# A two-layer MetaFormer kernel: three of layer 0's 56 expert tiles stand in a branch

## Chip, cores and metric

The kernel runs on one core of a Trainium2 chip. The metric is the device time of one execution in microseconds (us), as a median of several runs. Engines are named as in the profile: PE (TensorE matmul), PEld (its weight load), DVE (VectorE), ACT (ScalarE), POOL (GpSimd), SP (SyncE, which here issues nearly all plain DMAs). A q behind a name (POOLq) is that engine's sequencer.

## What is computed

The reference is a network of two layers on an input x of shape 2 x 256 x 56 x 56. Each layer adds a token mixer and then a mixture of experts. Layer 0's mixer is a windowed attention, layer 1's a pair of ternary 3x3 convolutions with batch norm. The change touches only layer 0's mixture of experts, in which every one of the 6272 tokens goes to two of eight experts:

```python
logits = tokens @ router_w.T
probs = softmax(logits)
rw, re = top_k(probs, 2)             # two experts per token
rw = rw / max(rw.sum(-1), 1e-12)
combine = zeros(N, 8).at[n, re].set(rw)
out = tokens
for e in range(8):
    h = gelu(tokens @ w1[e] + b1[e])  # 256 -> 256
    y = h @ w2[e] + b2[e]             # 256 -> 256
    out = out + combine[:, e:e+1] * y
```

All inputs come from a fixed seed, so the number of tokens that each expert gets is fixed too.

## The kernel before

**The tiles.** The router writes each token's row (and its number) twice to a DRAM tensor `xs`, into the region of its expert, by an indirect DMA. The experts then work on tiles of G = 256 rows of one expert. How many tiles an expert needs is known only from the counts, so the program has a fixed number of tile bodies, NTILE = (2·6272 + 8·255) // 256 = 56, which is enough for any counts. Which expert and which rows a body works on is read at run time from a table `where`. The table is made in two parts: part 0 (27 tiles, `EARLY[0]`) from the counts of the first strips, part 1 (29 tiles) when all counts are known. `planning` makes part 1 on DVE; in it, `end` holds the running sum of tiles over the experts, so that its last entry is the number of tiles that part 1 needs. Bodies beyond the last needed tile are executed all the same: their mask `held` is zero everywhere, the target row of every row becomes `FAR`, and the scatter with its bounds check writes nothing.

**One tile** is five steps in `experts_in_order`. `fetch_rows(j)`: SP reads a register from `where` and loads 256 rows (`xg`). `fetch_weights(j)`: SP reads a register and loads the expert's two weight matrices and biases (`w`, 641 KB; four buffers). `turn(j)`: PE transposes the rows into `pt`, ACT copies them to `ut`; DVE makes the target rows `dest` and `to`. `first(j)`: PE multiplies into `ph` (L1187), ACT applies the GELU to get `h` (L1194). `second(j)`: PE multiplies into `py` (L1206), DVE adds the bias to get `y` (L1216), and POOL scatters two blocks of 128 rows into `ys` by indirect DMA (L1218).

**The order.** The loop over tiles is software-pipelined by hand: rows are fetched four tiles ahead, weights three, `turn` two and `first` one. The order written in the source is the order on SP, PE, DVE and ACT (`manual_schedule` over these four engines); POOL's instructions are placed by the framework's scheduler, in their data order. After each tile the loop calls `beside(j)`, which advances other work that is hidden beside the experts: the ternary quantization of layer 1's convolution weights (`ternary`, DVE and ACT, L1402 to L1413), and, at j = NTILE - 2, three loads of `x_mid` (L1829) for the next stage.

**Behind the tiles** comes the start of layer 1. `combine(i)` gathers for strip i the two expert outputs of each token from `ys` (`got`, L1254), adds them up with the gates (L1270 on DVE; L1263 and L1266 on ACT and POOL for one strip), normalizes and transposes, and the first convolution (L1928) starts. The gathers read all of `ys`, so the first of them waits for the last scatter.

At its very end the kernel has one branch already: `either` reads a flag on every engine (L2401) and jumps over a general fallback program (L2402) if the flag is 0, which it is here.

## Time and profile before

| | |
|---|---|
| median of 3 runs | 1740.41 us (1736.08 to 1745.44) |
| the profiled execution | 1737.13 us, of which the span from first to last instruction is 1735.3 us |
| granted TensorE clock, mean | 0.899 |
| PE busy | 1507.6 us (87% of the span) |
| DVE / ACT / POOL busy | 957.5 / 692.9 / 636.8 us |
| experts of layer 0, first to last `py` | 505.4 us to 789.6 us |
| first `got` of layer 1's start | issued at 794.97 us |

The profile gives for each engine a list of instructions with start and duration, and for each idle stretch what ended it. The stage table gives, for chosen stretches of time, each engine's busy time, the granted clock and what the DMA engines moved. A busy engine is not by itself a bound: what a change in one stage is worth is read from the chain of waits there.

### The profile page before, as it was taken

What the parts mean: (1) busy time and instruction counts of PE and PEld (TensorE: products, weight loads), DVE (VectorE), ACT (ScalarE), POOL (GpSimd) and SP (SyncE); (2) the same over time, 40 slices, a digit from 0 to 9 for tenths busy, and PEclk for the clock granted to TensorE, in tenths of its full rate; (3) what the DMA queues carried; (4) which work ended last, traced back from release to release, by engine and by line L of the source; (5) the groups of instructions that cost most, each with busy time, mean ns of one, the idle gap of its engine ahead of it and who ended that gap; (6) DMA issues with size and microseconds to landing.
All of it is one profiled execution on the core that took longest, in us unless ns stands there. A gap on an engine that the chain in (4) does not pass through costs nothing. (4 is left out here: it accounts for less than half of the span.)

```text
span 1735.3 us, 25573 instructions
## 1 busy us (share of the span) xinstructions
PE 1507.6 (87%) x8445; PEld 1176.0 (68%) x8445; DVE 957.5 (55%) x2620; ACT 692.9 (40%) x1419; POOL 636.8 (37%) x728
## 2 busy tenths in 40 slices
PE   5999998999878788894989879957769999999964
PEld 3555565556557667783768768746658888888852
DVE  3456667466635335885999888777622212111136
ACT  2544443444323324544444263235423334343323
POOL 2111436235333653552333323427715542222210
PEclk9999999999879999996999989955579999999975
DMA  7112334112257769794441000024357777888858
GB/s 241 42 64 90 111 102 145 60 62 80 80 181 248 249 203 322 258 331 176 170 170 70 1 1 0 10 65 141 126 198 274 271 258 262 282 288 288 293 198 317
DMA packets 94157, 291.78 MB, mean 168 GB/s; under 512 B 20151, under 2 KB 35611, under 8 KB 84928
## 3 DMA queue, kind: packets, MB, share of 16 engines
q1 hardware_dynamic: 70384, 231.82, 40.3%
q0 software_dynamic: 19824, 51.82, 7.9%
q10 hardware_dynamic: 3808, 6.42, 1.0%
q8 instruction: 69, 1.13, 0.3%
q14 instruction: 72, 0.59, 0.1%
HBM read 218.55 MB, written 74.20 MB: 169 GB/s over the span
## 5 line engine op out<-in xcount | busy, mean ns | idle before, releaser
L1187 PE MATMUL ph<-ut,w 128*128 128x256 f32 (+1 forms) x1472 | 311.8, 363 | 18.5 <-DMA w<-in_L_experts 10.0
L1216 DVE TENSOR_TENSOR y<-py,w 128x512 f32<-128x512 f32 (+1 forms) x120 | 76.8, 640 | 412.5 <-PE py L1206 341.4
L1206 PE MATMUL py<-w,h 128*128 128x256 f32 x1288 | 300.5, 381 | 3.4 <-DVE y L1216 2.5
L1187 PEld LDWEIGHTS ph<-ut,w 128*128 128x128 f32 x1472 | 251.4, 195 | 49.6 <-DMA w<-in_L_experts 10.3
L1206 PEld LDWEIGHTS py<-w,h 128*128 128x128 f32 x1288 | 244.5, 192 | 37.1 <-DVE y L1216 2.9
L934 POOL DMA_INDIRECT xs<-u,pos x196 | 194.0, 990 | 127.9 <-issue 43.1
L1218 POOL DMA_INDIRECT ys<-y,dest x136 | 137.0, 1008 | 233.0 <-DVE dest L1162 100.4
L1194 ACT ACTIVATE h<-ph,w 128x256 f32<-128x256 f32 (+1 forms) x368 | 162.6, 448 | 119.0 <-PE ph L1187 91.5
L1597 ACT ACTIVATE ex<-sc 112x476 f32<-112x476 f32 (+3 forms) x224 | 116.9, 573 | 177.6 <-PE sc L1587 169.8
L1159 ACT COPY ut<-pt 128x512 f32<-128x512 f32 (+1 forms) x120 | 65.1, 543 | 293.1 <-PE pt L1155 258.2
L1928 PE MATMUL pc<-lo,wq 128*128 128x448 f32 x336 | 131.8, 394 | 5.7 <-DVE lo L1903 5.4
L1617 DVE TENSOR_TENSOR acc<-av,acc 128x238 f32<-128x238 f32 (+3 forms) x224 | 88.1, 408 | 82.9 <-PE av L1607 74.7
L1928 PE MATMUL pc<-hi,wq 128*128 128x448 f32 x336 | 131.0, 392 | 2.5 <-DVE x L1950 1.9
L1607 PE MATMUL av<-ex,vals 112*64 112x238 f32 (+3 forms) x896 | 126.9, 407 | 4.0 <-DVE acc L1617 4.0
L1218 POOL DMA_INDIRECT ys<-y,to x81 | 81.7, 1009 | 121.9 <-DVE dest L1162 63.4
L2071 PE MATMUL pc<-hi,wq 128*128 128x448 f32 (+1 forms) x288 | 102.5, 366 | 18.1 <-ACT hi L2038 9.4
L1578 PE MATMUL sc<-q_im,keys 32*112 32x238 f32 (+3 forms) x896 | 99.2, 423 | 7.9 <-ACT ex L1597 7.8
L2071 PE MATMUL pc<-lo,wq 128*128 128x448 f32 (+1 forms) x288 | 101.8, 363 | 0.2 <-DVE lo L2039 0.2
L1155 PE MATMUL pt<-ident,xg 128*128 128x128 f32 x434 | 71.2, 285 | 33.6 <-DMA xg<-xs 25.5
L1901 POOL TENSOR_TENSOR v<-pad 128x928 f32<-128x928 f32 (+1 forms) x28 | 56.7, 2035 | 103.5 <-ACT pad L1884 59.5
L1607 PEld LDWEIGHTS av<-ex,vals 112*64 112x64 f32 x896 | 57.3, 143 | 53.5 <-issue 30.0
L1155 PEld LDWEIGHTS pt<-ident,xg 128*128 128x128 f32 x434 | 56.5, 148 | 48.8 <-DMA xg<-xs 22.5
(278 smaller groups left out, 2474.5 us busy)
## 6 DMA issues: line engine op xcount, KB each, us to landing
w<-in_L_experts SPq DMA_DIRECT2D x64, 1154.0 KB
w<-in_L_experts SPq DMA_DIRECT2D x56, 641.0 KB
xg<-xs SPq DMA_DIRECT2D x97, 260.0 KB
acc<-in_fresh SPq DMA_DIRECT2D x14, 896.0 KB
got<-ys SPq DMA_DIRECT2D x21, 512.0 KB
got<-ys SPq DMA_DIRECT2D x7, 1024.0 KB
xt<-in_x_tok SPq DMA_DIRECT2D x14, 448.0 KB
rec<-shares SPq DMA_DIRECT2D x28, 224.0 KB
```

The source lines that it names most:

```text
L934: w = nc.gpsimd.indirect_dma_start(xs[:, :], bass.IndirectOffsetOnAxis(ap=pos[:, j, t0 + t : t0 + t + 1], axis=0), at_of[t][0][:, at_of[t] ...
L1155: nc.tensor.transpose(pt[:, k, i * P : (i + 1) * P], d["xg"][:, i, k * P : (k + 1) * P], ident)
L1187: nc.tensor.matmul(ph[:, :g], w1[:, k, f * P : (f + 1) * P], d["ut"][:, k, :g], start=k == 0, stop=k == KC - 1,)
L1194: nc.scalar.activation(d["h"][:, f, :g], ph[:, :g], AF.Gelu, bias=b1[:, f : f + 1])
L1206: nc.tensor.matmul(py[:, i, :], d["h"][:, f, i * P : (i + 1) * P], w2[:, f, :], start=f == 0, stop=f == NF - 1,)
L1218: o = nc.gpsimd.indirect_dma_start(ys[:, :], bass.IndirectOffsetOnAxis(ap=d["to"][:, i : i + 1], axis=0), y[:, i, :], None, bounds_check=T ...
L1578: nc.tensor.matmul(sc[h // 2][:, h % 2, :nq], keys[g][p, c, tx * TT : (tx + 1) * TT], q_im[p, c, r0:r1, c0:c1], start=True, stop=False,)
L1597: nc.scalar.activation(e[:, :, :nq], sc[j][:, :, :nq], AF.Exp, scale=HD**-0.5)
L1607: nc.tensor.matmul(av[VW * i : VW * (i + 1), :nq], vals[g % 3][:, tx, 2 * c + j, 2 * i : 2 * i + 2, :].rearrange("p a d -> p (a d)"), ex[j ...
L1617: added = nc.vector.tensor_tensor(d, av[:, :nq].rearrange("p (h w) -> p h w", w=c1 - c0), d, ALU.add)
L1928: nc.tensor.matmul(pc[:, :NT], wq[:, k, c, dx * C + o * P : dx * C + (o + 1) * P], part[:, :, k, dx : dx + W], start=m == 0, stop=m == 2 * ...
L2071: nc.tensor.matmul(pc[:, : 2 * ns * W], wq[:, k, c, dx * C + o * P : dx * C + (o + 1) * P], part[:, : 2 * ns, k, dx : dx + W], start=m == ...
```

## The change

The loop over layer 0's tiles stops after 53 of the 56 bodies. The last three stand in a branch behind it, written without the software pipeline. A new one-element tile `spare` is computed in `planning`: it is 1 if part 1 needs more than 29 - 3 = 26 tiles, that is, if the counts reach the 54th tile. Every engine reads `spare` into a register and branches on it. If the branch isn't taken, each engine runs a short block of semaphore operations in its place (each engine waits that its own earlier work is done and then adds to its semaphores what the three tiles would have added), so that later waits see the same counts either way. The three loads of `x_mid` move from j = 54 to j = 51.

```diff
+SPARE = 3
@@ in planning
             end = table("end", E)
             nc.vector.tensor_reduce(end, ends, AX.X, ALU.add)
+            if part == 1 and not halves:
+                spare = rt.tile([1, 1], I32, tag="spare", name="spare", bufs=1)
+                nc.vector.tensor_scalar(
+                    spare, end[0:1, E - 1 : E], float(n - SPARE), None, ALU.is_gt
+                )
+                spares.append(spare)
             yield
@@ in experts
             steps = experts_in_order(layer, FF, plans, ys, wp, at_tile)
             next(steps)
             steps.send((tp, ps))
+        more = nc.values_load_multi_w_load_instructions(spares[0], min_val=0, max_val=1)[1][0]
+        with tc.If(more > 0):
+            finish(steps)
@@ in experts_in_order
-        for j in range(len(tiles)):
-            if j + ROWS_AHEAD < len(tiles):
+        n = len(tiles) if layer else NTILE - SPARE
+        for j in range(n):
+            if j + ROWS_AHEAD < n:
                 fetch_rows(j + ROWS_AHEAD)
-            if j + AHEAD < len(tiles):
+            if j + AHEAD < n:
                 fetch_weights(j + AHEAD)
-            if j + 2 < len(tiles):
+            if j + 2 < n:
                 turn(j + 2)
-            if j + 1 < len(tiles):
+            if j + 1 < n:
                 first(j + 1)
             second(j)
             if at_tile is not None:
                 at_tile(*((j, 3) if layer else (j,)))
         yield
+        for j in range(n, len(tiles)):
+            fetch_rows(j)
+            fetch_weights(j)
+            turn(j)
+            first(j)
+            second(j)
@@ in beside
-            if j == NTILE - 2:
+            if j == NTILE - SPARE - 2:
                 for i in range(X_FIRST):
                     nc.sync.dma_start(XT[STRIPS[i]], by_token(x_mid, i))
```

On the engines the built program differs only around this place. SP reads `spare` right behind the planning, ahead of its first read of part 1's `where`, and branches when it has issued the `x_mid` loads. PE, DVE and ACT read `spare` and branch when their part of tile 52, the 53rd, is issued. POOL reads it and branches between the scatters of tile 51 and those of tile 52: tile 52's two scatters stand behind the branch. ACT's two copies of the ternary weights (L1413), which stood before `ut` of tile 55, stand behind the branch. The skipped block is short: 16 instructions on POOL, 14 on ACT, 19 on DVE, 45 on PE, 37 on SP. The block that the kernel's old last branch skips has 208 on POOL, 2453 on ACT, 3579 on DVE and 8261 on PE.

More of the change, by code (lines that the diff above doesn't have):

```diff
@@ L773, in scaled @@
             )
-    pace, spread = [], []
+    pace, spread, spares = [], [], []
     def routing(layer, wp, tp, ps):
```

## Prediction

> **What bounds the kernel at this place.** I read the stage table first, around the end of layer 0's tiles:

> ```profile
> core 0: us, PE busy (x) PEld busy (x) DVE busy (x) ACT busy (x) POOL busy (x), PEclk, DMA share, GB/s
> ...
> 745.00:784.00 39.00, 37.30 (x192) 32.50 (x190) 32.70 (x86) 19.73 (x36) 20.80 (x22) 1.00 0.92 315
> ...
> 784.90:794.90 10.00, 4.71 (x22) 3.80 (x20) 1.38 (x2) 0.95 (x2) 4.56 (x5) 0.95 0.02 0
> ...
> 797.00:820.00 23.00, 7.87 (x25) 4.56 (x26) 16.73 (x48) 14.32 (x32) 3.71 (x2) 0.50 0.66 260
> ```

> Up to 784 PE is the bound (37.3 of 39.0 us, clock 1.00), with the DMA engines close behind. In the ten us before 794.9 nothing is moved at all (0 GB/s), though four scatters are issued in them: the last tiles write no rows. Then comes a thin stage in which PE hardly works: DVE and ACT prepare the first strips of layer 1.

> Next the timeline of those us, engine by engine:

> ```profile
> 776.51 1.89 PE L1206 MATMUL py<-w,h 128*128 128x256 f32 x8
> ...
> 780.41 1.89 PE L1206 MATMUL py<-w,h 128*128 128x256 f32 x8
> ...
> 785.99 3.62 PE L1206 MATMUL py<-w,h 128*128 128x256 f32 x16
> ...
> 808.62 1.68 PE L1283 MATMUL pu<-ident,xn 128*128 128x128 f32 x6 [19.01 <-ACT xn L767]
> ...
> 779.50 4.12 ACT L1413 CAST sums<-x 128x2304 bf16<-128x2304 f32 x2 [2.31 <-DVE x L1410]
> ...
> 778.44 0.69 DVE L1216 TENSOR_TENSOR y<-py,w 128x512 f32<-128x512 f32 x1 [0.18 <-PE py L1206]
> ...
> 799.36 2.07 DVE L1270 SCALAR_TENSOR_TENSOR x<-got,wgt,x 128x256 f32<-128x256 f32 x5 [9.02 <-DMA got<-ys]
> ...
> 776.99 0.98 POOL L1218 DMA_INDIRECT ys<-y,to  x1 [0.30 <-issue]
> ...
> 779.41 0.97 POOL L1218 DMA_INDIRECT ys<-y,to  x1 [1.44 <-DVE y L1216]
> ...
> 780.69 0.98 POOL L1218 DMA_INDIRECT ys<-y,to  x1 [0.30 <-issue]
> ...
> 792.73 0.98 POOL L1218 DMA_INDIRECT ys<-y,to  x1 [0.30 <-issue]
> ...
> 794.97 1.29 SPq L1254 DMA_DIRECT2D got<-ys  x3
> ```

> Counting back from the end, the `py` at 785.99 is tiles 54 and 55, 780.41 is 53 and 776.51 is tile 52. The chain runs: last `y`, last scatter (ends 793.71), 1.26 us until SP may issue the gather (794.97), gather lands, DVE starts (799.36), and PE, idle for 19.01 us, starts at 808.62. So whatever moves the last scatter moves everything behind it.

> **Is the branch taken?** The counts follow from the reference's fixed inputs: the eight experts get 1527, 1691, 1588, 1573, 1468, 1602, 1515 and 1580 rows, hence 6+7+7+7+6+7+6+7 = 53 tiles. Part 1 needs 53 - 27 = 26, and 26 > 26 is false: not taken. The nearest a count comes to a step is 9 rows (1527 of 1536), far more than rounding moves. The 0 GB/s row says the same. Tile 52 holds only the last 1580 - 6·256 = 44 rows.

> **What is removed.** Three bodies, tiles 53 to 55. A body costs PE 3.9 us (776.51 to 780.41), so 11.7 us of PE; and ACT's 4.12 us `sums` copies, which delayed `ut` of tile 55, no longer stand in front of a tile. I don't add these up but take the chain: tile 52's scatters end at 780.69 + 0.98 = 781.67 in the old trace and nothing ahead of them changes. The old last one ended at 793.71. That is 12.04 us.

> **The landing.** The old last scatter was empty and took 1.26 us from its end to the gather's issue. Tile 52's carries 44 rows. Lower bound 1.26 us; upper bound 3.2 us, since all traffic had ceased by 784.9 although 1.3 MB of `x_mid` loads were in the queues with it. Those loads now come some 11 us earlier, so I take 1.5, near the lower. Gather at 783.2 in place of 794.97: 11.8 us gained.

> **The branch on each engine.** The old trace has no such short jump, but it has the kernel's last branch:

> ```profile
> L2401 POOLq TENSOR_LOAD <-flag x1: 492/492/492, 1671.7 to 1671.7; - x1
> ...
> L2402 POOLq COMPARE_BRANCH  x1: 57/57/57, 1672.3 to 1672.3; - x1
> ...
> L2402 POOLq EVENT_SEMAPHORE  x1: 17/17/17, 1672.8 to 1672.8; - x1
> ...
> L2402 DVEq COMPARE_BRANCH  x1: 72/72/72, 1727.5 to 1727.5; - x1
> ...
> L2402 DVEq EVENT_SEMAPHORE  x1: 21/21/21, 1731.1 to 1731.1; - x1
> ...
> L2402 PEldq COMPARE_BRANCH  x1: 3710/3710/3710, 1728.8 to 1728.8; - x1
> ```

> POOL, jumping over 208 instructions, has its next instruction 0.5 us after the branch; DVE over 3579 needs 3.6 us, PE over 8261 3.7 us, and ACT over 2453, in rows of the same view, 3.1 us. [...]

> - POOL is the only engine on the path: its branch stands ahead of tile 52's scatters. Its sequencer runs ahead of the engine (its last `ys` scatter in the trace starts at 1672.7, behind the branch at 1672.3). It is free at the latest when tile 51's second scatter ends, 777.97, and probably some 2 us earlier. Load 0.49, compare 0.06, jump 0.5, some four waits 0.3 and a second jump out of that block 0.1 to 0.5: 1.5 to 1.9 us, so 777.5 to 779.8 against the 779.41 at which `y` lets the scatter go. Exposed: 0 to 0.4; I take 0.1. The waits there are for scatters of tile 50 and before, issued 3.5 us or more earlier. [...]
> - PE branches after 778.4 and is next wanted some 19 us later; load 1.08 (PE's row at L2401) and 3.7 at worst are covered. DVE branches at about 779.5 (`y`, then the last ternary step) and is wanted when the gather lands, about 787.6: 0.54 + 0.07 + 3.6 = 4.2 at worst, covered. ACT branches at about 777.2; the `sums` copies then take their 4.1 us to about 784, and ACT is next wanted around 791 (803.13 in the old trace). SP branches at about 766, as soon as its last loads are out, 17 us before the gather. The gather also waits for the semaphores that PE, DVE and ACT add in their short blocks: at worst 783.7 (DVE), 0.5 us late; at 0.5 a jump, nothing.
> - SP's extra register read stands before the first `where` of part 1. It is covered by the planning itself: `end` is ready at 644.6, `where` at 650.2. DVE's one-element compare in that chain costs about 0.1 us, uncovered, since PE waits for the rows after it.

> **What moves.** The `x_mid` loads go out behind the weights of tile 52, at about 764.2 instead of 775.76, into a stage at 92% DMA share. They are 1.3 MB, at 315 GB/s 4.2 us of traffic; in exchange 2.7 MB of rows and weights of the three tiles are gone. The weights of tile 52 are issued ahead of them at 763.80 and used at 774.78. I cost this at nothing; the cover is 11 us.

> **Sum.** -11.8 + 0.1 (compare) + 0.1 (POOL) = -11.6 us against the profiled execution, span 1735.3 (1737.13 in all): 1725.5. That execution lies 3.3 us below the median of 1740.41; for the median I forecast 1740.4 - 11.6 = 1728.8. The stages behind only shift: PE's idle gap and the clock of 0.50 behind it stay as they are.

> **Rivals.** A difference of 0.5% (8.7 us) is about what a measurement of this kernel can tell from no change.
> [...]
> [...]
> 3. *The change doesn't do what it says*, and the branch is taken: three unpipelined bodies, each about 0.6 (transpose) + 0.6 + 1.9 + 0.9 (GELU) + 1.9 = 5.9 us, and tile 52's scatters behind theirs: about 28 us from 778.4 to the gather in place of 16.6, 11 us slower, 1751. The counts exclude it nearly.

> **Chances.** Forecast (gain above 8.7) 0.67; rival 1 and other partial losses 0.24, all within 0.5%; rival 2 0.07; rival 3 0.02. Runs scatter by some 5 us to either side. The range 1723 to 1737 holds the forecast with that scatter and all of rival 1.

> **What would show it.** After: no `py` behind 778.4 until layer 1, the first gather near 783, DVE's first add near 787.6, PE's first transpose near 797. [...] A PE wait for weights near 774.8 would mean the moved loads. I am wrong if the gather comes later than 787.

## The result and the profile after

The changed kernel takes 1727.12 us (median of 8 runs, 1721.83 to 1744.10) against 1739.11 us for the kernel before on the same chip (8 runs, 1735.97 to 1745.44). The ratio is 0.9936, with a 95% interval of 0.9912 to 0.9960: 11 us faster, 7 to 15 by the interval. The forecast was 1728.8. The profiled execution has 1724.05 us (forecast 1725.5), a span of 1722.3, against 1735.3 before.

First the stage table around the end of layer 0's tiles, after:

```profile
core 0: us, PE busy (x) PEld busy (x) DVE busy (x) ACT busy (x) POOL busy (x), PEclk, DMA share, GB/s
735.00:774.00 39.00, 37.53 (x190) 32.59 (x188) 34.30 (x87) 16.16 (x38) 20.51 (x22) 1.00 0.87 308
774.10:782.10 8.00, 0.00 (x0) 0.00 (x0) 2.22 (x5) 4.12 (x2) 3.24 (x4) 0.69 0.11 39
784.20:807.20 23.00, 7.83 (x25) 4.55 (x26) 16.70 (x48) 14.31 (x32) 3.66 (x2) 0.50 0.67 261
```

The three stages are those of before: PE-bound tiles, a stretch without matmuls, the thin start of layer 1. Only the middle one is different. No matmul is in it any more, so the branch was not taken, and POOL works for 3.24 of its 8 us.

Then the timeline of that stretch (start, duration, engine; in brackets the idle time before and what ended it):

```profile
766.90 1.89 PE L1216 MATMUL py<-w,h 128*128 128x256 f32 x8
768.62 1.89 PE L1197 MATMUL ph<-ut,w 128*128 128x256 f32 x8
770.35 3.62 PE L1216 MATMUL py<-w,h 128*128 128x256 f32 x16
795.84 1.68 PE L1300 MATMUL pu<-ident,xn 128*128 128x128 f32 x6 [21.88 <-ACT xn L768]
...
768.82 0.69 DVE L1226 TENSOR_TENSOR y<-py,w 128x512 f32<-128x512 f32 x1 [0.33 <-PE py L1216]
...
772.28 0.69 DVE L1226 TENSOR_TENSOR y<-py,w 128x512 f32<-128x512 f32 x1 [0.42 <-DMA ys<-y,to]
...
774.77 0.69 DVE L1423 TENSOR_TENSOR x<-x,low 128x512 f32<-128x512 f32 x1
775.38 0.68 DVE L1226 TENSOR_TENSOR y<-py,w 128x512 f32<-128x512 f32 x1
...
786.58 2.07 DVE L1287 SCALAR_TENSOR_TENSOR x<-got,wgt,x 128x256 f32<-128x256 f32 x5 [10.19 <-DMA got<-ys]
...
774.72 0.98 POOL L1228 DMA_INDIRECT ys<-y,to  x1 [0.30 <-issue]
778.37 0.97 POOL L1228 DMA_INDIRECT ys<-y,to  x1 [2.68 <-DMA ys<-y,to]
779.65 0.98 POOL L1228 DMA_INDIRECT ys<-y,to  x1 [0.31 <-issue]
...
782.17 1.34 SPq L1271 DMA_DIRECT2D got<-ys  x3
```

The chain is the forecast one: last `y`, last scatter, landing, gather at 782.17, first add at 786.58, first transpose at 795.84. All three are 12.8 us earlier than before. But the scatter that opens tile 52 starts at 778.37, though its `y` is done at 776.06: POOL was idle 2.68 us. The label says that a DMA ended this wait. What stood there is seen in POOL's sequencer rows of the branch line:

```profile
L1107 POOLq TENSOR_LOAD <-spare x1: 497/497/497, 773.5 to 773.5; - x1
...
L1108 POOLq EVENT_SEMAPHORE  x3: 17/42/43, 774.3 to 775.3; - x3
...
L1108 POOLq COMPARE_BRANCH  x1: 57/57/57, 774.1 to 774.1; - x1
L1108 POOLq INC_SWDGE_SEM  x1: 2109/2109/2109, 775.4 to 775.4; - x1
```

The jump is cheap: 0.14 us lie between the end of the compare and the first record of the short block. The waits for earlier scatters end at 775.34; the last of them is for tile 50's second scatter, whose last part lands at 775.28. Then a single instruction, INC_SWDGE_SEM, takes 2109 ns. At its end, from 777.42 to 777.47, six of the semaphores that count POOL's scatters go up, as many as there are skipped scatters. Tile 52's scatters stand behind it: the first starts 0.88 us after its end.

**The stage as a sum.** Executions differ in when they reach this place, for reasons far ahead of it (spare1, late_steps and move_only below, which ran on one chip and differ little up to here, have tile 50's `y` at 769.79, 773.22 and 776.73). So I count from the start of tile 50's `y` (770.66 before, 768.82 after) to the issue of the first gather, and call this the stage. The line of before from which it is counted:

```profile
770.66 0.69 DVE L1216 TENSOR_TENSOR y<-py,w 128x512 f32<-128x512 f32 x1 [0.32 <-PE py L1206]
```

Each row below is one profiled execution; the runs are those of the next section.

| us | tile 50's y to tile 52's y | to the start of the last scatter | to the gather | stage |
|---|---|---|---|---|
| before | 7.78 | 14.29 | 2.24 | 24.31 |
| after | 6.56 | 4.27 | 2.52 | 13.35 |
| no_branch | 6.55 | 2.24 | 2.51 | 11.30 |
| pool_last | 7.35 | 2.24 | 2.51 | 12.10 |
| pool_last2 | 6.56 | 2.24 | 2.51 | 11.31 |
| pool_far | 6.55 | 6.15 | 2.51 | 15.21 |
| taken | 6.55 | 19.18 | 2.50 | 28.23 |
| late_steps | 5.18 | 3.07 | 2.51 | 10.76 |
| best | 5.18 | 3.06 | 2.51 | 10.75 |
| loads_first | 10.44 | 3.43 | 2.51 | 16.38 |

Where two runs differ in nothing that bears on the stage, it repeats to 0.01 us: no_branch and pool_last2, late_steps and best, and before and move_only (24.31 both). So tenths of a us can be read in it, though not in the medians. The one exception is pool_last, for a wait that is shown there.

The gain of the change here is 24.31 - 13.35 = 10.96 us, in line with the 11 us of the ratio. The other 1.84 of the 12.8 us lie ahead of the stage, within that wander. Behind it nothing is gained: from the first add to the end it is 935.7 us, and 935.9 before.

### The profile page after: what moved, and what is told of

Same layout as the page of the kernel before. It is cut to its first block, busy times and chain, and to the rows that moved or that the text cites. A ratio compares the mean times of both kernels' runs of the same rounds, so it can differ in the third digit from the quotient of the medians.

```text
span 1722.3 us, 25393 instructions
## 1 busy us (share of the span) xinstructions
PE 1495.7 (87%) x8385; PEld 1164.4 (68%) x8385; DVE 953.5 (55%) x2609; ACT 689.0 (40%) x1410; POOL 631.1 (37%) x722
## 5 line engine op out<-in xcount | busy, mean ns | idle before, releaser
L1197 PE MATMUL ph<-ut,w 128*128 128x256 f32 (+1 forms) x1448 | 304.8, 361 | 13.4 <-DMA w<-in_L_experts 11.1
L1216 PE MATMUL py<-w,h 128*128 128x256 f32 x1264 | 296.4, 382 | 8.1 <-DVE y L1226 4.0
L1197 PEld LDWEIGHTS ph<-ut,w 128*128 128x128 f32 x1448 | 246.7, 195 | 43.1 <-DMA w<-in_L_experts 12.3
L1216 PEld LDWEIGHTS py<-w,h 128*128 128x128 f32 x1264 | 240.0, 192 | 42.5 <-DVE y L1226 4.4
L1228 POOL DMA_INDIRECT ys<-y,to x75 | 75.9, 1012 | 117.8 <-DVE dest L1172 63.7
```

What stands on the lines that cost most here:

```text
L1197: nc.tensor.matmul(ph[:, :g], w1[:, k, f * P : (f + 1) * P], d["ut"][:, k, :g], start=k == 0, stop=k == KC - 1,)
L1216: nc.tensor.matmul(py[:, i, :], d["h"][:, f, i * P : (i + 1) * P], w2[:, f, :], start=f == 0, stop=f == NF - 1,)
L1228: o = nc.gpsimd.indirect_dma_start(ys[:, :], bass.IndirectOffsetOnAxis(ap=d["to"][:, i : i + 1], axis=0), y[:, i, :], None, bounds_check=T ...
```

## Experiments

The median of the kernel before lies between 1720.56 and 1749.12 us in these groups of runs. So each ratio is to the kernel before on the same chip in the same group.

**no_branch: the branch is taken out, 53 bodies stand alone.**

```diff
-        more = nc.values_load_multi_w_load_instructions(spares[0], min_val=0, max_val=1)[1][0]
-        with tc.If(more > 0):
-            finish(steps)
```

It covers no counts beyond the 53rd tile.

> The changed kernel without its branch: neither the read of the flag nor the block of three bodies is in the program, 53 bodies stand alone. Measured by the stage from the start of tile 52's first y to the start of its last scatter (2.25 us before, 4.27 us changed). The prediction's own step (POOL loses 0.1 us): 4.2 us, gather where the changed kernel has it, time within 0.3 us of it. Theory A, POOL's short block (two waits, then 2.1 us in the instruction that brings the count of its DMA queue up to that of the skipped scatters) is on the chain: 2.2 to 2.5 us, gather and all behind it about 2 us earlier, time about 2 us less, which the time alone can hardly show. Rival B, tile 52's scatters are late by their queue and not by the branch: stage stays at 4.2 us. In neither does the stretch from tile 50's y to tile 52's (6.56 us) change, if what shortened it by 1.2 us is the absence of tiles 53 to 55; if the branch did that, it goes back to 7.8.

Measured: ratio to before 0.9901 (0.9866 to 0.9935). The timeline:

```profile
751.02 0.69 DVE L1223 TENSOR_TENSOR y<-py,w 128x512 f32<-128x512 f32 x1 [0.32 <-PE py L1213]
...
757.57 0.68 DVE L1223 TENSOR_TENSOR y<-py,w 128x512 f32<-128x512 f32 x1
...
758.53 0.97 POOL L1225 DMA_INDIRECT ys<-y,to  x1 [0.64 <-DVE y L1223]
759.81 0.97 POOL L1225 DMA_INDIRECT ys<-y,to  x1 [0.30 <-issue]
...
762.32 1.28 SPq L1268 DMA_DIRECT2D got<-ys  x3
```

The scatter now waits for `y` and not for a DMA, and 2.24 us lie between tile 52's `y` and the last scatter, as for this tile before. Theory A holds, rival B falls: the branch costs POOL 2.03 us (4.27 - 2.24), and nothing else in the stage. The 6.55 us from tile 50 to tile 52 stay, so that part of the gain belongs to the absent tiles and not to the branch.

**pool_last: POOL reads the flag and branches behind tile 52's scatters.**

```diff
-        more = nc.values_load_multi_w_load_instructions(...)[1][0]
+        with tc.issue_after(scatter[0]):
+            more = nc.values_load_multi_w_load_instructions(...)[1][0]
```

> The changed kernel with POOL's read of the flag and its branch ordered behind tile 52's two scatters; nothing else moves. Theory A (the 2.1 us are a fixed price of the instruction that corrects the queue's count, paid on POOL's sequencer): tile 52's scatters start right behind y, the stage from y to the last scatter is 2.3 us in place of 4.27, and the 2.1 us run beside the landing of the scatters; gather 1 to 2 us earlier than in the changed kernel counted from tile 52's y (5.0 to 5.8 us in place of 6.79). Rival C (that instruction waits until what was queued before it has landed, and its time only stretches with that): it now stands behind the landing of the last scatter, and the gather comes at 6.8 us or later behind y, no gain, or up to 1 us of loss. By the prediction's step (0.1 us) no difference: 6.8 us.

```profile
L1109 POOLq COMPARE_BRANCH  x1: 57/57/57, 765.6 to 765.6; - x1
L1109 POOLq INC_SWDGE_SEM  x1: 2157/2157/2157, 766.0 to 766.0; - x1
```

Measured: 0.9885 (0.9853 to 0.9918), and in a second run, pool_last2, 0.9921 (0.9899 to 0.9944). INC_SWDGE_SEM still takes 2157 ns, but from 766.0, while the last scatter (766.01) is carried out and lands. From tile 52's `y` to the gather it is 4.75 us instead of 6.79, the same as without any branch. So the price is one of POOL's sequencer, and hidden where no scatter is queued behind it. It is hidden narrowly: it ends at 768.18, and the last scatter lands at 768.26. For this reason the run alone does not refute rival C, a wait that lasts until the scatters have landed. Two other runs do. In pool_far the last scatter ahead of the instruction has landed at 757.33, and the instruction still takes 2122 ns from 757.43. In loads_first it is over at 794.19, before the scatter issued ahead of it lands (794.49 to 794.69).

The stage is 12.10 and not 11.30 because PE stopped once, at tile 52's weights:

```profile
756.94 1.97 PE L1198 MATMUL ph<-ut,w 128*128 128x256 f32 x8 [0.55 <-SPq L1109]
```

The label names SP's short block, which waits for the same semaphore; in the landing records (the trace notes when the parts of a transfer arrive) these weights were complete at 756.80. This was not expected; the last experiments ask where it comes from.

**pool_far: 600 one-element memsets on POOL inside the untaken block.** They are jumped over, not executed.

```diff
         with tc.If(more > 0):
             finish(steps)
+            for _ in range(600):
+                nc.gpsimd.memset(far_pad, 0.0)
```

> The changed kernel with 600 one-element memsets on POOL put into the block that is never taken: POOL's jump passes over 600 more instructions, they are not executed. [...] If the distance does not matter, nothing changes.

```profile
L1110 POOLq EVENT_SEMAPHORE  x4: 17/30/43, 757.1 to 757.3; - x4
...
L1110 POOLq COMPARE_BRANCH  x1: 57/57/57, 754.3 to 754.3; - x1
...
L1110 POOLq INC_SWDGE_SEM  x1: 2122/2122/2122, 757.4 to 757.4; - x1
```

Measured: 0.9934 (0.9909 to 0.9960). From the compare's end to the next record it is 2.74 us, in place of 0.14: with 600 more instructions to pass, POOL's jump takes 2.6 us longer. Why is not shown. It lies between two jumps of the kernel's last branch in before, counted alike: 0.44 us over 208 instructions (POOL) and 3.00 over 2453 (ACT). INC_SWDGE_SEM's 2.1 us come on top of it, and the stage is 1.86 us longer than in the changed kernel: the waits for earlier scatters, which took 1.04 us there, are over by now, and the rest of the jump is exposed. The medians don't resolve 1.9 us.

**taken: the comparison's constant is one lower, so that the three bodies run.**

```diff
-                    spare, end[0:1, E - 1 : E], float(n - SPARE), None, ALU.is_gt
+                    spare, end[0:1, E - 1 : E], float(n - SPARE - 1), None, ALU.is_gt
```

> The comparison's constant is one lower, so that the branch is taken with the same data: the three bodies run, with rows that count for nothing, on one side of a jump and without the overlap with tiles before. The prediction's rival 3: 28 us from 778.4 to the gather in place of 16.6, 11 us slower than the kernel before, some 24 us slower than the changed one (1751). If the bodies overlap among themselves as those before do (3.9 us a tile on PE), the loss is only the fill of the pipeline, about 6 us against the kernel before, 1746.

```profile
762.89 0.68 DVE L1226 TENSOR_TENSOR y<-py,w 128x512 f32<-128x512 f32 x1
...
767.18 0.69 DVE L1226 TENSOR_TENSOR y<-py,w 128x512 f32<-128x512 f32 x1 [2.20 <-PE py L1216]
772.20 0.69 DVE L1226 TENSOR_TENSOR y<-py,w 128x512 f32<-128x512 f32 x1 [3.79 <-PE py L1216]
777.27 0.69 DVE L1226 TENSOR_TENSOR y<-py,w 128x512 f32<-128x512 f32 x1 [4.38 <-PE py L1216]
...
784.57 1.36 SPq L1271 DMA_DIRECT2D got<-ys  x3
```

Measured: 1.0018 (1.0000 to 1.0037), 1724.23 against 1721.09 us, 0.2% slower than before and at the edge of what can be told from nothing. Both numbers that I had given are too high: rival 3's 11 us and the 6 us of overlapped bodies. A body takes 5.0 us (from `y` to `y`), not 5.9, and the first follows tile 52 by 4.29 us. Tile 52's `y` to the gather is 21.7 us in place of 16.5 before, 5.2 more; the 1.2 that the stage gains ahead of it go off. That is +3.9 in the stage and 3 in the medians. With counts that reach the 54th tile, then, the change loses some 4 us, against the 11 that it wins if they don't. What real rows in the three bodies would add is not shown, since here they carry none.

**spare1: one tile in the branch instead of three.**

```diff
-SPARE = 3
+SPARE = 1
```

> The changed kernel with one tile in the branch in place of three: tiles 53 and 54 run in the pipeline with no rows, tile 55 alone stands in the block, which is not taken. It skips two scatters in place of six. Theory A1, the correction of the DMA queue's count is a fixed price: its row shows 2.1 us as before. Theory A2, it goes with the number of skipped scatters: 0.7 us. Of the 13.0 us that the absence of three tiles takes from the stretch between tile 50's y and the gather (24.3 to 11.3 us), a third stays: 4.3 gained, 2.0 (A1) or 0.6 (A2) lost on POOL, so 22.0 us (A1) or 20.6 us (A2); time 2 to 4 us below before.

```profile
L1108 POOLq INC_SWDGE_SEM  x1: 2186/2186/2186, 783.1 to 783.1; - x1
```

Measured: 0.9983 (0.9965 to 1.0001). For two skipped scatters the instruction takes 2186 ns, for six 2109 to 2157: a fixed price (A1). Yet the stage is 20.45 us, the number of A2 and not the 22.0 of A1, so the arithmetic from price to stage was wrong. The rest of the timeline shows what was left out:

```profile
781.02 0.69 DVE L1226 TENSOR_TENSOR y<-py,w 128x512 f32<-128x512 f32 x1 [2.42 <-issue]
785.75 0.69 DVE L1226 TENSOR_TENSOR y<-py,w 128x512 f32<-128x512 f32 x1 [4.04 <-PE py L1216]
```

The last `y` comes at 785.75, INC_SWDGE_SEM is over at 785.3. Here PE is late with its last tile (it waits 2.20 us for the GELU, and its last `py` then takes 2.53 us in place of 1.89), and POOL's 2.1 us lie within that wait. The price is fixed; what of it is exposed depends on when the last `y` comes.

**late_steps and best: also the DVE steps between the last two `y` later.** In the changed kernel PE has finished tile 52 at 773.97, but DVE takes four steps of the ternary weights first (the last at 774.77) and `y` starts at 775.38.

```diff
-                for _ in range(4):
+                for _ in range(4 if j != NTILE - SPARE - 2 else 0):
```

> Two changes against the changed kernel: POOL's read and branch behind tile 52's scatters (as in pool_last), and the four steps of the ternary weights that DVE does between tile 51's y and tile 52's y are left to the steps behind the tiles. Theory 1, y of tile 52 (ready on PE some 1.2 us before DVE takes it) is what the last scatters wait for: tile 52's y starts 1.2 us earlier and the gather comes up to 1.2 us earlier than without, so 10.1 us after tile 50's y in place of 11.3. Theory 2, POOL's own scatters are next: the second scatter of tile 51 is issued 1.28 us ahead of the earliest start of tile 52's first, so that only 0.3 us are gained, 11.0 us from tile 50's y to the gather, and the wait of 0.64 us of tile 52's first scatter for y is down to 0.3.

The lines of best, which has the edits of late_steps:

```profile
762.65 0.69 DVE L1227 TENSOR_TENSOR y<-py,w 128x512 f32<-128x512 f32 x1 [0.21 <-PE py L1217]
764.38 0.69 DVE L1227 TENSOR_TENSOR y<-py,w 128x512 f32<-128x512 f32 x1 [1.03 <-PE py L1217]
...
764.89 0.97 POOL L1229 DMA_INDIRECT ys<-y,to  x1 [0.30 <-issue]
766.16 0.98 POOL L1229 DMA_INDIRECT ys<-y,to  x1 [0.30 <-issue]
767.44 0.97 POOL L1229 DMA_INDIRECT ys<-y,to  x1 [0.30 <-DMA ys<-y,to]
```

Measured for late_steps: 0.9927 (0.9906 to 0.9949). Tile 52's `y` is 1.37 us earlier, the gather only 0.54: theory 2. POOL's four scatters now follow each other without a gap, 1.28 us apart, so they are the bound. The wait for `y` fell to 0.30 as expected; the other 0.2 us come from tile 51's second scatter, 1.28 instead of 1.47 us behind its first.

best was to have the `x_mid` loads behind the branch as well:

> late_steps (POOL's branch behind tile 52's scatters, the four DVE steps between the last two y left for later) with the x_mid loads behind the branch. From tile 50's y to the gather 10.7 to 10.8 us as in late_steps, whatever the loads cost, since late_steps showed no wait for weights; against the kernel before 24.3 - 10.75 = 13.5 us less, ratio about 0.992, against 0.9936 for the changed kernel.

Measured: 0.9907 (0.9885 to 0.9930), stage 10.75 us. The loads have no part in this, since their edit did nothing, as the next run shows (here they go out at 752.73, ahead of SP's branch at 754.9). It is a second run of late_steps, and with it the shortest stage of all, 2.6 us under that of the changed kernel. The ratios of these versions and of the changed kernel overlap; only the stage tells them apart.

**loads_late, pool_last2: is it the moved loads that made PE wait?**

```diff
-            if j == NTILE - SPARE - 2:
-                for i in range(X_FIRST):
-                    nc.sync.dma_start(XT[STRIPS[i]], by_token(x_mid, i))
 ...
         experts(0, C, plans0, ys[0], wp0, tp0, ps0, beside)
+        for i in range(X_FIRST):
+            nc.sync.dma_start(XT[STRIPS[i]], by_token(x_mid, i))
```

> pool_last (POOL's branch behind tile 52's scatters) with the x_mid loads issued behind the branch instead of directly behind tile 52's weights. The changed kernel and the variants have them 0.4 us behind those weights, which land 5.2 to 6.9 us after their issue; the use on PE comes about 6.2 us after it, and in pool_last PE waited 0.55 us. Theory L, the loads share the DMA engines with these weights and eat the cover: here the weights land 4.0 to 5.0 us after their issue, PE shows no wait, and the stretch from tile 50's y to the gather is 11.3 us as in no_branch (12.1 in pool_last). Prediction's step (the loads cost nothing, the wait in pool_last came from other traffic): weights land in 5 to 7 us as before, no change. The loads themselves must still land before the first add, some 15 us after tile 50's y; if they do not, the add starts more than 4.6 us after the gather.

Inconclusive. The loads are still issued 0.38 us behind tile 52's weights (748.86 after 748.48) and ahead of SP's branch: the written place did not change the queue. So it is pool_last once more (0.9920, 0.9895 to 0.9945), with a stage of 11.30.

> pool_last once more, unchanged, to see how firm its stage is: from tile 52's y to the gather 4.75 us again (POOL's branch is off the chain), and from tile 50's y to tile 52's y 6.55 us where PE does not wait for tile 52's weights, up to 7.4 us where it does (7.35 the first time). Theory L and its rival both allow either value here; 6.55 would say that the wait is a matter of the run.

Stage 11.31, no wait for weights. The wait in pool_last is thus a matter of the single run; whether the moved loads make it more likely is not shown. By the landing records tile 52's weights were complete ahead of their first matmul by 0.71 us in the changed kernel, 1.08 in no_branch, 1.67 in pool_far, 0.25 in taken, 1.97 in late_steps, 1.53 in pool_last2, 0.29 in loads_late and 0.67 in best, and too late in pool_last. In the kernel before it was 1.00 us (769.89 to 770.89), so the moved loads did not visibly take the margin.

**move_only: the kernel before with the loads at tile 51.**

```diff
-            if j == NTILE - 2:
+            if j == NTILE - 5:
```

> The kernel before, with nothing changed but the place of the x_mid loads: they are issued at tile 51, as in the changed kernel, in place of tile 54; all 56 tiles run, no branch. The prediction's step (moved loads cost nothing): PE waits for no weights, the stretch from tile 50's y to the first gather stays at 24.3 us, time as before. Rival: they push the weights of tile 52 and of the tiles behind it back by their own 4.2 us of traffic; then PE shows a wait for w and the stretch grows to up to 28.5 us. A gain is possible too: if what the gather waits for at the end includes the landing of these loads, the stretch shrinks by up to 1 us.

Measured: 0.9994 (0.9974 to 1.0014); tile 50's `y` to the gather 24.31 us (776.73 to 801.04), as before; no wait for weights. But it says less than it should: here weights of later tiles still pace SP's queue, and the loads go out 1.2 us behind tile 50's `y` (5.1 behind it before), while in the changed kernel they go out 6.5 us ahead of it. It prices a smaller move.

**loads_first: the loads directly ahead of tile 52's weights.**

```diff
-            if j == NTILE - SPARE - 2:
+            if j == NTILE - SPARE - 5:
```

> The changed kernel with the three x_mid loads issued directly ahead of tile 52's weights on SP's queue instead of directly behind them; nothing else changes. The prediction costed the moved loads at nothing and named 11 us of cover between the issue of these weights and their use. In six runs of the changed kernel and its variants those weights landed 0.3 to 2.0 us before PE used them, once 0.4 us too late. Theory L (the cover is those 0.3 to 2.0 us, and loads that get in front cost their traffic, 1.3 MB at some 315 GB/s, 4.2 us, plus 1.4 us of issue): PE waits 3 to 5 us for w ahead of tile 52's first matmuls, the stretch from tile 50's y to tile 52's y grows from 6.56 to 9.5 to 11.5 us, and the gather follows; time 3 to 5 us above the changed kernel, near 0.996 of before. The prediction's step (11 us of cover): no wait, 6.56 us.

```profile
775.60 0.34 SPq L1155 DMA_DIRECT2D w<-in_L_experts  x1
...
784.40 2.57 PE L1197 MATMUL ph<-ut,w 128*128 128x256 f32 x8 [1.97 <-DMA w<-in_L_experts]
786.76 4.75 PE L1216 MATMUL py<-w,h 128*128 128x256 f32 x16
```

And the stage table of the same kernel, in the tiles and behind PE's wait:

```profile
770.00:784.00 14.00, 12.43 (x64) 10.61 (x62) 12.92 (x32) 4.60 (x9) 7.69 (x8) 1.00 0.90 322
784.40:791.51 7.11, 7.10 (x24) 5.62 (x24) 2.73 (x5) 0.95 (x2) 1.79 (x3) 0.76 0.11 39
```

The weights are issued at the same place as in the changed kernel (6.87 us ahead of tile 50's `y`) but land 8.3 us after the end of their issue instead of 5.6. PE waits 1.97 us, less than the 3 to 5 of theory L, and then works at a granted clock of 0.76: the last `ph` takes 2.57 for 1.89 us, the `py` of tiles 51 and 52 4.75 for 3.62. Tile 50 to tile 52 grows by 3.88 us, and the gather by 3.03, since part of POOL's correction now falls into the delay. The stretch of 10.44 us lies in theory L's 9.5 to 11.5, though nearly half of the growth is the slower clock and not the wait. What the stage shows is that loads in front do delay tile 52, so the cover of these weights is far less than 11 us. The time did not show it: 0.9913 (0.9883 to 0.9942) is no loss against the changed kernel, and misses the 0.996 that I had expected. With six executions of it and a wander of several us ahead of the stage, I go by the stage and leave the median unexplained.

## Why the prediction was right, step by step

- **Not taken:** right; no matmul between 774 and 795. **The chain from last `y` to gather, and the later stages only shifting:** right; add and transpose moved with the gather to 0.02 us.
- **Three bodies, 12.04 us:** right as the difference between the last scatters. "Nothing ahead of them changes" was wrong by 1.22 us in favour: tile 50's `y` to tile 52's is 6.56 us for 7.78. Early steps of the absent tiles no longer stand between the last `py` (lines below).
- **Landing:** 1.5 us forecast, 1.54 measured (780.63 to 782.17). Against before that is 0.28 more, 0.24 forecast.
- **POOL's branch:** this is the mis-sized term. Forecast 0 to 0.4 us exposed, 0.1 taken; measured 2.0. Of the parts that were listed, load (0.50) and compare (0.06) are right, the jump is too high (0.14 for 0.5), the second jump (0.1 to 0.5) has no row (the next record stands 0.04 us behind the short block), and the waits are too low (1.04 for 0.3, since tile 50's second scatter had not landed). All these are over at 775.39, when tile 52's `y` has just begun, and would have cost nothing. The part that was not listed is INC_SWDGE_SEM, 2.1 us. The short block was counted as "some four waits 0.3", and no row of before has a block that skips POOL's own scatters (the fallback's rows were read only for the jump). That the 0.5 us of the row over 208 instructions hold for a jump over 16 was an estimate, and no run shows it: the changed kernel has 0.14. Nor does any run show a loss on POOL that fills the range up to 1737: it is 2.03 us here (4.27 - 2.24), and 3.91 in pool_far (6.15 - 2.24).
- **The other engines' branches:** covered, as forecast. DVE takes 0.72 us from its compare to the next record, some 10 us ahead of the gather's landing. Behind the gather nothing is exposed: from it to the first add it is 4.41 us (4.39 before), to PE's first transpose 13.67 (13.65). The compare of `spare` takes 0.14 us (0.1 forecast) and SP's extra read 0.48, and neither shows a cost: `end` to `where` takes 5.67 us, and 5.81 before.
- **The moved loads, at nothing:** right in effect, wrong in the reason. "The cover is 11 us" reads a wrong line: the `ph` at 774.78 is tile 53's. Tile 52's is the one at 770.89 in the lines below, whose weight load waits for the semaphore of the transfer issued at 763.80. Issue to use was thus 7.1 us, of which the transfer took 6.1: 1.00 us was left before, and 0.71 is left in the changed kernel. In one of the nine executions with the loads behind these weights that are listed above nothing was left, and PE waited 0.55 us.
- **Rival 3's price:** 11 us forecast, 3.9 in the stage; bodies on one side of a jump overlap more than was assumed (5.0 us a body for 5.9).

Between the `py` of tiles 50, 51 and 52 the kernel before has these lines:

```profile
768.73 1.89 PE L1206 MATMUL py<-w,h 128*128 128x256 f32 x8
770.46 0.60 PE L1155 MATMUL pt<-ident,xg 128*128 128x128 f32 x4
770.89 1.89 PE L1187 MATMUL ph<-ut,w 128*128 128x256 f32 x8
772.62 1.89 PE L1206 MATMUL py<-w,h 128*128 128x256 f32 x8
774.35 0.60 PE L1155 MATMUL pt<-ident,xg 128*128 128x128 f32 x4
774.78 1.89 PE L1187 MATMUL ph<-ut,w 128*128 128x256 f32 x8
```

The two `pt` are the `turn` of tiles 53 and 54, the last `ph` is the `first` of tile 53; only the `ph` at 770.89 is tile 52's own. Without them PE does the `py` of tiles 51 and 52 without a break (770.35, 3.62 us, x16) and is 2.6 us ahead. DVE, with its four ternary steps between the two `y`, takes 1.4 of that back; late_steps has it all (5.18 us). no_branch has the 6.55 us too.

The sum: -12.04 - 1.22 + 2.02 + 0.28 = -10.96 us, forecast -11.6. Two misses of 1.2 and 1.9 us, of opposite sign, hid each other. The mechanism was right; that the sum came so close was luck.

## What to carry over

When a block with scatters is skipped, look at what the engine must do in its place to keep the counts (2.1 us on POOL here), not only at the jump (0.14), and let that engine branch behind the last work that others wait for (4.75 us from the last `y` to the gather in pool_last, 6.79 in the changed kernel). Taking three tiles off the end of this pipelined loop gained 1.22 us more than their own 12.04, since their early stages stood between the last tiles. And cover is counted from a transfer's landing to its use (1.00 us for tile 52's weights before), not from its issue (7.1); in a pipelined loop it takes care to find the use that belongs to the transfer.

## What the runs showed of the hardware

```profile
784.16 1.99 PE L1187 MATMUL ph<-ut,w 128*128 128x256 f32 x8 [1.86 <-ACT ut L1159]
```
